# First attention stripes of a four-layer graph stack: the last group's rows, its left and right factors, and the distance behind GpSimd

## The chip, the cores and the metric

The kernel runs on one core of a Trainium2 chip. The metric is the time of one execution on the device in microseconds (us); the median of three runs of the kernel before is 1066.32 us (1062.9 to 1067.3). In this text PE is TensorE (matrix products), DVE is VectorE, ACT is ScalarE, POOL is GpSimd, and SP issues the loads. PSUM is the memory that PE writes its products to, and SBUF is the working memory.

## The reference

A graph of 4096 nodes with 64 features each goes through four layers. The adjacency matrix `adj` (4096 x 4096, zeros and ones) is the same in all of them, and each layer ends in `x = layernorm(x + layer(x))`.

```python
# layer 0: mean over neighbours
h = (adj @ X + X) / clip(sum(adj, 1) + 1, 1)
out = relu(concat([X, h]) @ W + b);  out / max(norm(out), 1e-12)
# layers 1 and 3: hyperbolic attention (curvature c)
left, right = logmap0(x) @ w_att[:D], logmap0(x) @ w_att[D:]
att = sigmoid(left[:, None] + right[None, :] + b_att) * adj
support = einsum('ij,ijd->id', att, logmap(x[:, None], x[None, :]))
proj(expmap(x, support))
# layer 2: a decayed sum over the last neighbours of each row
w = mask * where(pos > 0, 0.5 ** (k - pos), 0);  w @ (x @ weight) + bias
```

In an attention layer every pair of nodes (i receives, j sends) has a weight, which depends on both nodes' rows, and `logmap(x_i, x_j)` is a combination of the two rows whose factors depend on their inner product and norms. So the work by pair is one scalar function of a few inner products, and then a matrix product.

## The kernel before, in words

**Tiles and stripes.** The 4096 nodes form four groups of 1024, taken in the order 3, 2, 1, 0; group 0 is the last. An attention layer has one stripe per group of receiving nodes. A stripe goes through sixteen steps g = 15 to 0, each of two blocks of 128 sending nodes. `load` brings 128 x 2048 values of `adj` for a step (1 MB).

**What a block costs.** For each block, PE fills a PSUM tile z (128 x 1024, two halves of 512, three such tiles in turn) with the sum of three products: the edges (L1143), `hi_lo` of the senders with `lo_hi` of the receivers (L1146), and `src` of the senders with `dst` of the receivers (L1149). ACT makes a sigmoid `sig` (L1161) and a square `sq` of z (L1164). DVE makes the product `t = max(z, 0) * sig` (L1167), and once per step a pass `t = (sq + c) * t` over both blocks, 128 x 2048 (L1170). PE adds t times the rows `xe` to `acc` (L1121), two steps later. `hi_lo` and `src` are called left factors here and `lo_hi` and `dst` right factors: the left ones of a group are used in every stripe, when its nodes send; the right ones only in the group's own stripe. The first stripe (group 3) comes to the senders of group 0 at g = 3, where `need((layer, 0))` asks for them.

**Row work.** Between two layers each group's rows have to be finished and prepared: in layer 0 `end_0` takes the sums by neighbour to rows (matmuls L1510 and L1511, one half of the group at a time or both; L1516 to L1519 finish a half), applies relu (L1523), and normalizes (sums of squares L1525 on POOL and L1527 on DVE, `rsqrt` L775 to L790, scaling and adding L1531 and L1532); `end_2` does the same for layer 2 (L1652 to L1668). Then `norm_rows` applies the layernorm (mean L924 and L925, centring and squares L929 and L930, variance L936 and L938, another `rsqrt`, L944 to L946), and `prepare` makes the factors: b and its reciprocal rb (L958 to L962), the scaled rows y (L967, L968), half-precision copies on ACT (L971 to L973), high and low parts (L975 to L987), `xe` (L994, L997), a third `rsqrt`, and the terms tt and q1 (L1006 to L1008). After that come the four turns, which are transposes on PE (L1023) and a copy on ACT (L1027) each, for hi_lo, lo_hi, src and dst; then two logarithms on ACT (L1031, L1032), the attention matmuls (L1036) and some fifteen small DVE operations, which give `left` and `right` (L1046 to L1073). For group 0 (`pooled` in the code) much of this runs on POOL instead of DVE, so `rsqrt` there is one DVE operation and ten small POOL operations.

**What sets the order.** Row work is written as generators in three queues. `tick` goes through them; it is called after every block and every pass in an attention layer (twice each time in the first stripe of layer 1, four times in that of layer 3), and four times per step in layer 0. A generator that yields n isn't gone on with for n ticks. `soon`, `near`, `after` and `far` give such distances; `far(small, large)` is the distance behind POOL, made from a count of small and of large operations. `need(tag)` ticks until a tag is done. In layers 0 and 2 the order on PE and ACT is that of the program text; in the attention layers the framework's scheduler sets it, and it may move an instruction ahead of the place where the text has it. `take` hands out a PSUM bank for the turns: a second bank (`spare`) is there in layer 0 only, and `spare_ends` closes it before layer 1 begins, when z needs the space. `free` waits until the bank has been given back.

In the kernel before, the last group's `end_0` starts in layer 0, and what is left of it is done under the first stripe of layer 1. The line that decides on one bank or two is

```python
for some in ((0, 1),) if spare else ((0,), (1,)):
```

Of the kernel before, what the change touches and what calls it, by code (L numbers as in the profile page):

```python
# [21 lines left out]
D = 64  # L22
# [39 lines left out]
def gnn_stack_kernel(  # L62
# [509 lines left out]
    def stream(fits):  # L572

        with ExitStack() as st:
# [10 lines left out]
            GROUPS = tuple(reversed(range(NW)))  # L585
# [8 lines left out]
            queues, place, done, held = ([], [], []), [0, 0], set(), []  # L594
# [22 lines left out]
            def tick(n):  # L617
                for _ in range(n):
                    place[1] += 1
                    mark(False)  # L620
                    for queue in queues:
                        while queue and queue[0][1] <= place[1]:
                            wait = next(queue[0][0], None)
                            if wait is None:
                                queue.pop(0)
                                continue
                            queue[0][1] = place[1] + wait
                            if wait:
                                break
                    mark(True)  # L630

            def later(steps, second=False, wait=0):
                queues[int(second)].append([steps, place[1] + wait])
# [10 lines left out]
            def need(tag):  # L644
                while tag not in done:
                    assert any(queues), tag
                    tick(1)
# [12 lines left out]
            def near():  # L660

                return 3 if place[0] == 0 else 1
# [7 lines left out]
            def far(small, large=0):  # L670

                beat = {1: 0.8, 3: 0.4}.get(place[0], 1.6)
                return 1 + int((small * 0.29 + large * 1.04 + 2.3) / beat)

            spare, turn_of = [], [0]

            def take(dtype, *shape):


                held.append(1)  # L680
                turn_of[0] += 1
                if not spare or turn_of[0] % 2:
                    return aux.tile(list(shape), dtype, name="aux")
                return spare[0](dtype, shape)
# [6 lines left out]
            def free():  # L691
                while held:
                    yield 1
# [22 lines left out]
            def grp(name, bufs=None):  # L716
                kw = {"bufs": bufs} if bufs else {}
                return row.tile([P, WB, D], F32, name=name, **kw)

            def nums(name, n=WB):  # L720
                return row.tile([P, n], F32, name=name)
# [81 lines left out]
            src = keep.tile([D + 10, N], F16, name="src")  # L803
# [23 lines left out]
            ys = keep.tile([P, WB, 3 * D + 10], F16, name="ys")  # L827
# [122 lines left out]
            def prepare(layer, s, att, b_att, curve, least, good, small):  # L950
# [5 lines left out]
                pooled = s == GROUPS[-1]  # L956
# [13 lines left out]
                def second():  # L970
# [38 lines left out]
                    by_log = layer == 3 and s != GROUPS[-1]  # L1009
                    if by_log:  # L1010
                        half_log_of_ratio(t, q1)
                    yield far(10, 1) if pooled else 2 * near()
                    for into, rows_of in (
                        (hi_lo, ys[:, :, : 2 * D]),
                        (lo_hi, ys[:, :, D : 3 * D]),
                        (src, ys[:, :, 2 * D :]),
                        (dst, yd),
                    ):
                        n = rows_of.shape[2]
                        yield from free()  # L1020
                        turned = take(F16, P, WW)
                        for k in range(WB):
                            nc.tensor.transpose(  # L1023
                                turned[:n, k * P : (k + 1) * P], rows_of[:, k, :], ident16
                            )
                        yield near()
                        nc.scalar.copy(into[:, cols], turned[:n])  # L1027
                        held.pop()
                        yield 1
                    if not by_log:  # L1030
                        nc.scalar.activation(t, t, AF.Ln, bias=1.0)  # L1031
                        nc.scalar.activation(q1, q1, AF.Ln, bias=1.0, scale=-1.0)  # L1032
# [30 lines left out]
                    if s == GROUPS[0]:  # L1063
                        yield from spread_left(s)
                    done.add((layer, s))

                    V.tensor_mul(own, own, own)
                    V.tensor_mul(g, rbg, rbg)
# [376 lines left out]
            with ExitStack() as lp:  # L1445
# [52 lines left out]
                def end_0(s, tops):  # L1498
                    z = grp("z0")
                    yield from free()  # L1500

                    for some in ((0, 1),) if spare else ((0,), (1,)):
                        ts = []
                        for h in some:
                            top, low = tops[h]
                            t = take(F32, P, SB, P)
                            for k in range(SB):
                                cols = slice(k * P, (k + 1) * P)
                                to = t[:, k, : D + 1]
                                nc.tensor.matmul(to, top[:, cols], sum_w, start=True, stop=False)  # L1510
                                nc.tensor.matmul(to, low[:, cols], count_w, start=False, stop=True)  # L1511
                            ts.append((h, t))
                        for h, t in ts:
                            at = slice(s * WB + h * SB, s * WB + (h + 1) * SB)
                            d = nums("deg", SB)
                            V.reciprocal(d, t[:, :, D])  # L1516
                            zz = z[:, h * SB : (h + 1) * SB, :]
                            V.tensor_mul(zz, t[:, :, :D], over(d))
                            V.tensor_add(zz, zz, xw[:, at, :])  # L1519
                        if some == (0,):  # L1520
                            yield near()
                    held.clear()
                    V.tensor_scalar(z, z, 0.0, None, ALU.max)  # L1523
                    sq, n2 = grp("sq"), nums("n2")
                    nc.gpsimd.tensor_mul(sq, z, z)  # L1525
                    yield 1
                    V.tensor_reduce(n2, sq, AX.X, ALU.add)  # L1527
                    V.tensor_scalar(n2, n2, 1e-24, None, ALU.max)
                    if s == GROUPS[-1]:
                        n = yield from Small(True, "").rsqrt(n2, "n", 0)  # L1530
                        nc.gpsimd.tensor_mul(z, z, over(n))  # L1531
                        nc.gpsimd.tensor_add(z, z, x0[:, blocks(s), :])  # L1532
                        yield far(10, 2)
                    else:
                        n = rsqrt(n2, "n")
                        yield 1
                        V.tensor_mul(z, z, over(n))
                        V.tensor_add(z, z, x0[:, blocks(s), :])
                        yield 1
                    yield from norm_rows(1, s, z, x2[:, blocks(s)])  # L1540
                    yield from prepare(
                        1, s, att1, batt1_sb, curve1, 1e-15, good[:, 0], 70
                    )

                with tc.manual_schedule(engines=FIXED):
                    for s in GROUPS:
                        sums = [ps.tile([P, W], F32, name="acc") for _ in range(2)]
                        counts = [ps.tile([P, W], F32, name="acc") for _ in range(2)]
                        parts = ((first, sums, P), (third, counts, D + 1))
# [34 lines left out]
                        for h in range(2):  # L1584
# [9 lines left out]
                            nc.scalar.copy(low, counts[h][: D + 1])  # L1594
                            tops.append((top, low))
                        later(end_0(s, tops))
                        if s > 0:
                            own_of = linear(0, s - 1, w0_sb[:D, :], own_part)
                            later(in_turn((0, s - 1), own_of))
# [11 lines left out]
            def attention(layer, curve, rates, behind):  # L1611

                need((layer, GROUPS[0]))
                for n, s in enumerate(GROUPS):
                    if n:
                        need((layer, s, "left"))
                    anchored[0] = n > 0
                    then = GROUPS[n + 1] if n + 1 < NW else None
                    sums = attend(layer, s, rates[n], then)
                    move_s = in_turn((layer, s, "moved"), move(layer, s, sums, curve))  # L1620
                    if n:
                        later(
                            in_turn((layer + 1, s + 1), there((layer, s + 1, "moved")), behind(s + 1)),
                            True, 9,
                        )
                    apart = 2 if n + 1 == NW and layer == 1 else 0
                    later(move_s, apart)
                    if n + 1 == NW:
                        later(in_turn((layer + 1, s), behind(s)), apart)
                anchored[0] = False  # L1630
# [188 lines left out]
            into = aux.tile([D, 1], F32, name="aux")  # L1819
# [22 lines left out]
    with tc.If(fit < P):  # L1842
        with ExitStack() as st:
# [6 lines left out]
            for t, w_att in ((att1_sb, w_att1), (att3_sb, w_att3)):  # L1850
                src = w_att.rearrange("a o -> o a")
# [38 lines left out]
```

## Time and profile before

| | us |
|---|---|
| median of three runs | 1066.32 |
| profiled execution, its own time | 1064.98 |
| its span in the profile | 1063.3 |
| stretch of layer 1's first stripe, from 186.30 | to 270.40 |
| group 0's row work on DVE in layer 3, from 718.48 | to 761.25 |
| one step of a later stripe, two products and a pass on DVE | 2 x 1.22 + 2.31 |

The busiest engine over the whole span is PE (93%), then DVE (85%), ACT (71%) and POOL (32%). Of the 40 slices of the span, each 26.6 us long, PE is below nine tenths in the first, the fourth, the seventh to the ninth (159.5 to 239.2 us), the twenty-eighth (717.7 to 744.3 us) and the last. A share of the span is a mean over four layers with different limits, so the question here is what the engines do in two places: from 186 us, where layer 1 begins, and from 715 us, where layer 3 does. In the views below, one line of the timeline is: start, duration, engine, line of the code, operation, result and operands with their shapes, how many of them, and in brackets the idle time before it and who ended that. A line of the waits is: what waited, for what, total, times, longest.

### The profile page before, as it was taken

Reading aid. Unit: us, or ns where it says so; the run is one execution under the profiler, and the core shown is the slowest. Engines: PE = TensorE matmul, PEld = TensorE weight load, DVE = VectorE, ACT = ScalarE, POOL = GpSimd, SP = SyncE. Lnnn points to the kernel's source line nnn. Section 1 sums busy time; section 2 is a strip of 40 time slices with the busy share of each in tenths; the row PEclk is TensorE's granted clock in tenths of the full one; section 3 lists DMA queues with packets and bytes.
Section 4 is the critical chain, followed back from the end, with each engine's and each line's share of the span. In section 5 each row is a group of like instructions: output and inputs, shape, how many; then the busy total and the mean of one; then the engine's idle time right before and its main releaser. Section 6 shows DMA issues by size and latency. Waiting matters only on the chain.

```text
span 1063.3 us, 13594 instructions
## 1 busy us (share of the span) xinstructions
PE 985.4 (93%) x4845; PEld 400.7 (38%) x4845; DVE 901.2 (85%) x1383; ACT 753.4 (71%) x876; POOL 339.1 (32%) x695
## 2 busy tenths in 40 slices
PE   4998998879999999999999999997999999999991
PEld 2454554323333333333333344442333333333330
DVE  6677878779999999999485579857899999999996
ACT  0013122859989888888677688896998888888970
POOL 0011222470064464455200020105401562573670
PEclk8999999989999999999999999998999999999996
DMA  8999999836665656566599999994465766665600
GB/s 338 369 420 367 389 390 387 336 107 222 216 220 198 238 204 232 198 224 219 218 331 341 372 357 314 322 328 179 163 240 194 245 226 209 237 218 198 228 3 22
DMA packets 38580, 271.62 MB, mean 255 GB/s; under 512 B 4710, under 2 KB 4710, under 8 KB 5734
## 3 DMA queue, kind: packets, MB, share of 16 engines
q1 hardware_dynamic: 37728, 270.03, 69.7%
q8 instruction: 40, 0.66, 0.2%
q10 hardware_dynamic: 774, 0.63, 0.2%
q14 instruction: 38, 0.31, 0.1%
HBM read 269.58 MB, written 1.05 MB: 255 GB/s over the span
## 4 chain that ended last, share of the span: by engine, by line
PE 66%; DVE 18%; POOL 5%; DMA 4%; ACT 4%; issue 2%; ACTq 0%; SPq 0%; POOLq 0%; DVEq 0%
PE acc L1121 18%; PE z L1743 11%; PE z L1143 8%; PE z L1149 8%; PE z L1146 7%; DVE t L1170 5%; DVE t L1167 5%; PE acc L1561 4%; DMA edges<-in_adj_dram 3%; PE z L1755 3%; DVE junk L871 2%; PE z L1709 2%; ACT sq L1750 1%; ACT sq L1164 1%; POOL sq L1525 1%
## 5 line engine op out<-in xcount | busy, mean ns | idle before, releaser
L1167 DVE SCALAR_TENSOR_TENSOR t<-z,sig 128x1024 f32<-128x1024 f32 x256 | 309.1, 1218 | 22.4 <-ACT sq L1164 19.8
L1164 ACT ACTIVATE sq<-z 128x1024 f32<-128x1024 f32 x256 | 255.4, 1022 | 62.1 <-PE z L1149 31.7
L1170 DVE SCALAR_TENSOR_TENSOR t<-sq,t 128x2048 f32<-128x2048 f32 x127 | 293.4, 2311 | 0.3
L1161 ACT ACTIVATE sig<-left_b,right 128x1024 f32<-128x1024 f32 x256 | 287.3, 1150 | 6.5 <-DVE t L1167 6.0
L1121 PE MATMUL acc<-t,xe 128*64 128x512 f32 x1024 | 261.5, 616 | 13.4 <-DVE t L1170 13.4
L1143 PE MATMUL z<-edges,two_i 128*128 128x512 bf16 x512 | 200.3, 391 | 6.2 <-DVE t L1167 6.2
L1149 PE MATMUL z<-dst,src 74*128 74x512 f16 x512 | 194.8, 380 | 0.0
L1146 PE MATMUL z<-lo_hi,hi_lo 128*128 128x512 f16 x512 | 193.7, 378 | 0.0
L1750 ACT ACTIVATE sq<-z 128x512 bf16<-128x512 f32 (+1 forms) x192 | 137.9, 741 | 39.5 <-PE z L1743 38.8
L1121 PEld LDWEIGHTS acc<-t,xe 128*64 128x64 f32 x1024 | 64.9, 138 | 144.4 <-issue 110.0
L871 DVE SCALAR_TENSOR_TENSOR t<-edges 128x2048 bf16<-128x2048 f32 x32 | 74.4, 2335 | 28.7 <-DMA edges<-in_adj_dram 28.6
L1561 PE MATMUL acc<-edges,first 128*128 128x512 bf16 x256 | 81.1, 398 | 18.1 <-DMA edges<-in_adj_dram 17.9
L1143 PEld LDWEIGHTS <-two_i 128*128 128x128 bf16 x512 | 50.3, 98 | 118.7 <-issue 73.1
L1743 PE MATMUL z<-edges,pass_by 128*128 128x512 bf16 x248 | 86.4, 388 | 6.3 <-ACT sq L1750 5.8
L1743 PE MATMUL z<-edges,enter 128*128 128x512 bf16 x256 | 88.2, 387 | 0.0
L871 DVE SCALAR_TENSOR_TENSOR junk<-edges 128x2048 bf16<-128x2048 f32 x32 | 73.1, 2284 | 14.9 <-DMA edges<-in_adj_dram 14.9
L1561 PE MATMUL acc<-edges,third 128*65 128x512 bf16 x256 | 80.5, 396 | 0.0
L1149 PEld LDWEIGHTS <-src 74*128 74x128 f16 x512 | 49.1, 96 | 73.5 <-issue 11.9
L1146 PEld LDWEIGHTS <-hi_lo 128*128 128x128 f16 x512 | 50.2, 98 | 63.7 <-issue 18.3
L1270 POOL TENSOR_TENSOR w_att<-x,u 128x512 f32<-128x512 f32 x6 | 18.2, 3028 | 169.9 <-ACT u L1264 169.9
L1709 PE MATMUL z<-sq,halves 128*128 128x512 bf16 x128 | 48.1, 377 | 0.6 <-ACT sq L1750 0.6
L1525 POOL TENSOR_TENSOR sq<-z 128x512 f32<-128x512 f32 x4 | 10.1, 2526 | 117.2 <-DVE z L1523 97.4
(466 smaller groups left out, 996.5 us busy)
## 6 DMA issues: line engine op xcount, KB each, us to landing
edges<-in_adj_dram SPq DMA_DIRECT2D x256, 1024.0 KB, 4.9
x<-in_x_dram SPq DMA_DIRECT2D x4, 256.0 KB
out_dram<-x ACTq DMA_DIRECT2D x2, 256.0 KB
out_dram<-x SPq DMA_DIRECT2D x2, 256.0 KB
w_sb<-in_L_gnn_W_dram ACTq DMA_DIRECT2D x1, 32.0 KB, 4.9
w_twice<-in_L_gnn_weight_dram ACTq DMA_DIRECT2D x2, 16.0 KB, 8.7
given<-in_L_gnn_b_dram ACTq DMA_DIRECT2D x1, 0.2 KB
given<-in_L_gnn_bias_dram ACTq DMA_DIRECT2D x1, 0.2 KB
```

The lines of the kernel that those rows point to most:

```text
L871: V.scalar_tensor_tensor(junk, a, 0.0, a, ALU.not_equal, ALU.not_equal, accum_out=odd[:, n : n + 1])
L1121: it = nc.tensor.matmul(acc[h * D : (h + 1) * D, :], xe[:, j, :], t[:, k, h * W : (h + 1) * W], start=j == BLOCKS[0], stop=j == BLOCKS[-1],)
L1143: nc.tensor.matmul(half, two_i, edge[:, at : at + W], start=True, stop=False)
L1146: nc.tensor.matmul(half, hi_lo[:, of], lo_hi[:, to], start=False, stop=False)
L1149: last = nc.tensor.matmul(half, src[:, of], dst[:, to], start=False, stop=True)
L1161: nc.scalar.activation(sig, left_b, AF.Sigmoid, bias=right[:, j : j + 1])
L1164: nc.scalar.activation(sq[:, k], zp, AF.Square, bias=ROOT + OFF, scale=-1.0 / UNIT)
L1167: V.scalar_tensor_tensor(ts[k][:, k], zp, 0.0, sig, ALU.max, ALU.mult)
L1170: V.scalar_tensor_tensor(t, sq, HIGH**2, t, ALU.add, ALU.mult)
L1561: nc.tensor.matmul(accs[h][:m], lhs[:, j, :], edge[:, at : at + W], start=j == BLOCKS[0], stop=j == BLOCKS[-1],)
L1743: nc.tensor.matmul(z[:, h : h + W], lhs, rhs[:, h : h + W], start=j == BLOCKS[0], stop=True, skip_group_check=True,)
L1750: weighed[0] = nc.scalar.activation(w, z[:, :n], AF.Exp, bias=-(OFF_EDGE + CUT) * LN2, scale=-LN2)
```

## The change

- The last group's `end_0` in layer 0 is now driven until both halves of its rows are out of PSUM (a new tag, `(0, s, "rows")`, and a `need` for it) while both banks are still there.
- The order of the four turns becomes hi_lo, src, lo_hi, dst, for all groups. For group 0 only the left factors, hi_lo and src, are turned at that place. Its logarithms, attention matmuls and terms follow, then the tag that the first stripe asks for; the right factors lo_hi and dst are turned behind it. A new tag, "turned", is asked for ahead of every stripe but the first.
- The distance `far` grows: its constant goes from 2.3 to 3.9 us, which is one tick more in layers 0 and 2, two in layer 1 and four in layer 3. Ahead of the turns its arguments go from 10 small and 1 large operations to 14 and 2.

```diff
@@ -670,7 +670,7 @@
             def far(small, large=0):
 
                 beat = {1: 0.8, 3: 0.4}.get(place[0], 1.6)
-                return 1 + int((small * 0.29 + large * 1.04 + 2.3) / beat)
+                return 1 + int((small * 0.29 + large * 1.04 + 3.9) / beat)
 
             spare, turn_of = [], [0]
 
@@ -1009,13 +1009,15 @@
                     by_log = layer == 3 and s != GROUPS[-1]
                     if by_log:
                         half_log_of_ratio(t, q1)
-                    yield far(10, 1) if pooled else 2 * near()
-                    for into, rows_of in (
+                    yield far(14, 2) if pooled else 2 * near()
+                    turns = [
                         (hi_lo, ys[:, :, : 2 * D]),
+                        (src, ys[:, :, 2 * D :]),
                         (lo_hi, ys[:, :, D : 3 * D]),
-                        (src, ys[:, :, 2 * D :]),
                         (dst, yd),
-                    ):
+                    ]
+
+                    def turn(into, rows_of):
                         n = rows_of.shape[2]
                         yield from free()
                         turned = take(F16, P, WW)
@@ -1027,6 +1029,9 @@
                         nc.scalar.copy(into[:, cols], turned[:n])
                         held.pop()
                         yield 1
+
+                    for parts in turns[:2] if pooled else turns:
+                        yield from turn(*parts)
                     if not by_log:
                         nc.scalar.activation(t, t, AF.Ln, bias=1.0)
                         nc.scalar.activation(q1, q1, AF.Ln, bias=1.0, scale=-1.0)
@@ -1063,6 +1068,10 @@
                     if s == GROUPS[0]:
                         yield from spread_left(s)
                     done.add((layer, s))
+                    if pooled:
+                        for parts in turns[2:]:
+                            yield from turn(*parts)
+                    done.add((layer, s, "turned"))
 
                     V.tensor_mul(own, own, own)
                     V.tensor_mul(g, rbg, rbg)
@@ -1520,6 +1529,7 @@
                         if some == (0,):
                             yield near()
                     held.clear()
+                    done.add((0, s, "rows"))
                     V.tensor_scalar(z, z, 0.0, None, ALU.max)
                     sq, n2 = grp("sq"), nums("n2")
                     nc.gpsimd.tensor_mul(sq, z, z)
@@ -1594,6 +1604,8 @@
                             nc.scalar.copy(low, counts[h][: D + 1])
                             tops.append((top, low))
                         later(end_0(s, tops))
+                        if s == GROUPS[-1]:
+                            need((0, s, "rows"))
                         if s > 0:
                             own_of = linear(0, s - 1, w0_sb[:D, :], own_part)
                             later(in_turn((0, s - 1), own_of))
@@ -1613,6 +1625,7 @@
                 need((layer, GROUPS[0]))
                 for n, s in enumerate(GROUPS):
                     if n:
+                        need((layer, s, "turned"))
                         need((layer, s, "left"))
                     anchored[0] = n > 0
                     then = GROUPS[n + 1] if n + 1 < NW else None
```

## The prediction

> **What bounds the kernel now.** I read the page's head, then the busy times of four stretches, then the waits and the timeline of the two that are not full. The head says that TensorE is the bound over the whole:
>
> ```profile
> span 1063.3 us, 13594 instructions
> PE 985.4 (93%) x4845; PEld 400.7 (38%) x4845; DVE 901.2 (85%) x1383; ACT 753.4 (71%) x876; POOL 339.1 (32%) x695
> ```
>
> The edits act where the two attention layers begin. Busy times by stretch (first stripe of layer 1, a later stretch of it, then the same for layer 3):
>
> ```profile
> core 0: us, PE busy (x) PEld busy (x) DVE busy (x) ACT busy (x) POOL busy (x), PEclk, DMA share, GB/s
> 186.30:270.40 84.10, 73.15 (x361) 28.98 (x362) 68.71 (x90) 69.32 (x74) 32.01 (x56) 0.96 0.59 213
> 270.40:347.00 76.60, 76.60 (x336) 27.15 (x335) 74.47 (x55) 67.91 (x73) 31.12 (x79) 1.00 0.63 218
> 720.00:790.00 70.00, 61.37 (x284) 22.48 (x283) 60.93 (x73) 58.77 (x64) 24.57 (x43) 0.95 0.55 193
> 790.00:870.00 80.00, 80.00 (x351) 28.14 (x349) 78.03 (x58) 71.16 (x75) 29.45 (x78) 1.00 0.61 211
> ```
>
> Later stretches have no PE idle at clock 1.00. The first stripes have 10.95 us (84.10 - 73.15) and 8.63 us, at 0.96 and 0.95: about 19.6 us is all that this change can address, plus the slow clock. PE there waits for DVE's products, and DVE for GpSimd. DVE's waits in 181 to 290 us (total, times, longest):
>
> ```profile
> DVE t L1167 <- ACT sq L1164: 6.8, 6, 4.0
> DVE rb L962 <- POOL b L959: 2.2, 1, 2.2
> DVE n_m L924 <- POOL z L1532: 2.1, 1, 2.1
> DVE n_v L936 <- POOL sq L930: 0.9, 1, 0.9
> ```
>
> The timeline, layer 1 and then layer 3, shows the chain behind them:
>
> ```profile
> 199.54 2.28 POOL L787 TENSOR_TENSOR rs_t<-n 128x8 f32<-128x8 f32 x1
> ...
> 230.44 1.03 PE L1023 MATMUL aux<-ident,ys 128*128 128x128 f16 x8 [4.14 <-POOL ys L987]
> 231.40 3.68 PE L1121 MATMUL acc<-t,xe 128*64 128x512 f32 x8
> ...
> 238.17 1.22 DVE L1167 SCALAR_TENSOR_TENSOR t<-z,sig 128x1024 f32<-128x1024 f32 x1 [4.02 <-ACT sq L1164]
> ...
> 737.57 0.20 DVE L962 RECIPROCAL rb<-b 128x8 f32<-128x8 f32 x1 [3.70 <-POOL b L959]
> ...
> 739.98 1.97 PE L1121 MATMUL acc<-t,xe 128*64 128x512 f32 x4 [3.82 <-DVE t L1170]
> ...
> 757.45 0.17 DVE L1054 SCALAR_TENSOR_TENSOR f<-q,tt 128x8 f32<-128x8 f32 x1 [1.30 <-ACT q L1032]
> ```
>
> PE's 4.14 us wait for ys becomes, a few instructions later, DVE's 4.02. GpSimd's small operation took 2.28 us instead of 0.20 because it lay under a DVE pass (L1170 at 199.48, also 2.28). Read off the timeline after product 0 (products are numbered from 0 in issue order), DVE idles 0.36 + 2.14 + 0.93 + 2.23 + 4.02 + 1.19 + 0.26 + 0.30 + 0.72 = 12.15 us in layer 1, and 1.22 + 3.70 + 0.40 + 1.30 + 0.74 + 0.99 = 8.35 us in layer 3. PE has no gap after 255.57 and 766.24.
>
> **What the Trainium skill says.** "SBUF — State Buffer", "SBUF: two separate sides": DVE and GpSimd share a port pair under a lock held for a whole instruction, so a DVE operation with two SBUF inputs shuts GpSimd out. The trace agrees (2.28 for 0.20). "TensorE: Matmul & The Clock Gate", "What's actually happening": the clock halves after some 3.4 us of idleness. Agrees: after 4.14 us idle the accumulation (L1121) takes 3.68 us for a usual 1.94, the next z block 1.23 for 0.66, 2.3 us more; after 3.82 us in layer 3 the same. "ScalarE: Activation LUTs", "What ACT_TABLE_LOAD costs": about 1.28 us for a load; the trace has 1.28 ahead of L1031. "PSUM — Partial Sum Buffer", "PSUM bank collisions raise a hardware error": engines on one bank are put in order. Agrees: sq ran 191.34 to 192.37, its product began at 192.40.
>
> **The change part by part.** What follows rests on the order in which each engine of the changed program issues its instructions, with the durations of the trace before. The counts are the same; nothing is removed but waits, and no DMA moves.
>
> Costing nothing: hi_lo, src before lo_hi, dst in layers 0 and 2 (the same 8 transposes and one 1.0 us copy each, under a PE that is full; exposed they would be equal too); the wait for "turned" of later groups (group 0's is turned by the tenth of a stripe's 16 steps, three stripes early); one tick more in layer 0.
>
> Layer 1, against before:
> 1. *Both halves from two banks.* The second half's matmuls (L1510/1511) now precede the first z block; they wait for ACT's last src copy (185.4). z starts at about 188.2 instead of 186.44, product 0 at 191.25 instead of 190.49: +0.76. Row operations that lay after product 0 (relu 0.34, n 0.60 net of overlap) leave, but some 0.2 returns as a longer sq wait: -0.75.
> 2. *L924 right behind product 0* (before: after product 4). GpSimd's ten rsqrt operations and two wide ones now have one product and no other cover; I get their end at 196.6, so the wait grows from 2.14 to 4.2: +2.06. PE idles about 4.5 us here, and its clock drops, but DVE is ahead with nothing yet owed.
> 3. *L936 after product 4*: its 0.93 goes. L962 keeps its two products and two passes of cover: 2.2, no change.
> 4. *Distance and order at the transposes.* ys's low part (L987) stands 3.6 us earlier on GpSimd, hi_lo's transposes (8, L1023) later: PE's 4.14 becomes 1.9, and the 4.02 of DVE goes: -4.02.
> 5. *Terms ahead of right factors.* Ln (L1031) now comes before the sq of product 16, and needs GpSimd's last small operation (L1007), which by the walk just misses a gap and lies under a pass: ACT stops, sq is behind it, DVE idles: +1.9. Product 17's 1.19 stays. The three small ones (1.28) become 0.35: -0.93.
>
> Sum: 0.76 - 0.75 + 2.06 - 0.93 - 4.02 + 1.9 - 0.93 = -1.9. The miss in step 5 is by 0.2 to 0.3 us, less than the walk's error; without it the 1.9 is gone and half of the 1.19: -4.4. I take the middle, -3.1.
>
> Layer 3: L936's 1.22 goes (product 3 is ahead of it); L962 has two products and a pass more of other work on DVE, 3.70 becomes 1.7: -2.0; 0.40 goes. Ln stands before the sq of product 14 and its input ends at about 758.85 while the table is loaded by 755.2: DVE waits 3.0 in place of 1.30: +1.7. The attention matmuls (L1036) need the one row bank that src's copy (763.45) still holds; z blocks are queued behind them on PE, which idles about 4.8; of this DVE sees 1.6 where it waited 0.74 + 0.99: -0.1. PE's slow clock then costs 2.3, of which I let 1.5 reach the end. Sum -1.2 - 2.0 - 0.4 + 1.7 - 0.1 + 1.5 = -0.5. Bounds: -5.0 without the Ln wait and the slow clock, +1.5 if the L962 wait stays. Group 0's left factors are needed at product 24; all this is done some four products earlier, so nothing is late next.
>
> Together -3.6: the profiled execution (1064.98, span 1063.3) would take 1061.4; it stood 1.3 below the median of the runs, so the median goes from 1066.32 to 1062.7. A measurement of this kernel can tell about 0.5% from no change: 1061.0 and 1071.7 are the marks.
>
> **Rivals.** *A, the chain slips between the passes.* No Ln wait in either layer: -4.4 - 5.0 = -9.4, 1056.9. For it: passes are only 2.28 of each 4.62 us step, and the early L987; against: eleven small operations in a row, each of which can meet a pass. *B, the slower side: GpSimd's lock, moved onto ACT.* Each further small operation under a pass costs 2.28 - 0.20 = 2.1, and where Ln waits, every later sq is behind it, with nothing in between. From the two sums (-2.4), one more collision is about even with before, and four more, two in each layer, pass the mark: +6.0, 1072.3. For it: the Ln waits are new, and L924 lost its cover. Against: collisions also go away with the order. *C, waits only change their names:* the row chain on GpSimd is as long as before, and where product 24 isn't waiting for it, distance without a shorter chain gives back later what it saves (4.02 saved, 2.06 + 1.9 paid): 1066. Against it: PE loses its slow stretch in layer 1's transposes.
>
> **How the numbers follow.** Forecast 0.34, A 0.30, C 0.16, B 0.20. Faster than 1061.0: nearly all of A (0.28) and the low edge of the forecast (0.08), 0.36. Slower: B, 0.19. The rest, 0.45. The range, 1055 to 1072, leaves out A's lowest tenth or two and half of B; the forecast's own is 1060 to 1065.5.
>
> **What would show it.** Right: the L924 wait near 4 us, no L936 wait, PE at L1023 (hi_lo, layer 1) below 2.5 us and L1121 behind it at 1.94, no 4 us wait of L1167; in layer 3 L962 near 1.7; new waits of ACT for L1007. Wrong towards A: no ACT waits for L1007, a first stripe of layer 3 with PE idle under 5 us. Wrong towards B: several GpSimd operations of 128x8 at about 2.3 us ahead of Ln, PE idle above 11 us in a first stripe. A change outside 181 to 256 and 718 to 778 us would overturn the whole.

## The result, and the profile after

| | before | after |
|---|---|---|
| median of 21 runs, us | 1066.99 (1062.9 to 1072.2) | 1062.45 (1059.0 to 1067.5) |
| profiled execution: own time, span, us | 1064.98, 1063.3 | 1063.81, 1062.1 |

The ratio of after to before is 0.9957, 95% interval 0.9942 to 0.9971: the change makes the kernel faster by 4.5 us, with 3.6 forecast. The two profiled executions stand only 1.2 us apart, and that difference has to be understood before anything is read from it. First the head of the page of after:

```profile
span 1062.1 us, 13509 instructions
PE 981.6 (92%) x4760; PEld 401.9 (38%) x4845; DVE 900.2 (85%) x1383; ACT 753.1 (71%) x876; POOL 339.0 (32%) x695
```

The counts of DVE, ACT and POOL are those of before. (PE has 85 records fewer, but as many weight loads: matmul records that are missing from the trace.) Then the busy times of the two first stripes, in the stretches that were shown of before:

```profile
core 0: us, PE busy (x) PEld busy (x) DVE busy (x) ACT busy (x) POOL busy (x), PEclk, DMA share, GB/s
186.30:270.40 84.10, 75.47 (x357) 29.24 (x364) 70.86 (x91) 71.59 (x77) 34.04 (x56) 0.94 0.61 221
720.00:790.00 70.00, 62.62 (x283) 23.32 (x287) 61.86 (x74) 59.64 (x64) 24.60 (x43) 0.95 0.53 185
```

PE's idle time went from 10.95 to 8.63 us and from 8.63 to 7.38 us, but its clock in layer 1 from 0.96 to 0.94: some idleness has become slow running. DVE's waits in 181 to 290 us, after:

```profile
DVE t L1176 <- ACT sq L1173: 5.2, 7, 1.6
DVE n_m L924 <- POOL z L1542: 3.8, 1, 3.8
DVE rb L962 <- POOL b L959: 2.2, 1, 2.2
```

The wait of L936 is gone, and the longest wait for a square fell from 4.0 to 1.6 us; L924's has grown from 2.1 to 3.8. (Behind the edit at L1009 the line numbers are up to 13 higher than before: the product L1167 is L1176 here, the pass L1170 is L1179, the turns L1023 are L1025, the logarithm L1031 is L1036.) The timeline of after, first layer 1 on PE, ACT and POOL, then layer 3:

```profile
198.67 0.61 PE L1152 MATMUL z<-edges,two_i 128*128 128x512 bf16 x1 [3.56 <-DVE t L1176]
...
201.35 3.05 PE L1130 MATMUL acc<-t,xe 128*64 128x512 f32 x8
...
225.59 0.40 PE L1025 MATMUL aux<-ident,ys 128*128 128x128 f16 x4 [1.51 <-POOL ys L987]
225.91 1.94 PE L1130 MATMUL acc<-t,xe 128*64 128x512 f32 x8
...
236.20 2.33 POOL L1006 TENSOR_TENSOR tt<-q,rt 128x8 f32<-128x8 f32 x1
...
238.89 0.21 ACT L1036 ACTIVATE tt<-tt 128x8 f32<-128x8 f32 x1 [2.24 <-POOL tt L1007]
...
739.16 0.20 DVE L962 RECIPROCAL rb<-b 128x8 f32<-128x8 f32 x1 [1.37 <-POOL b L959]
...
757.91 0.21 ACT L1036 ACTIVATE tt<-tt 128x8 f32<-128x8 f32 x1 [3.02 <-POOL tt L1007]
...
762.53 0.34 PE L1041 MATMUL aux<-att,hi_lo 128*128 128x7 bf16 x8 [2.90 <-ACT src L1029]
```

PE's wait for ys at the turns went from 4.14 to 1.51 us, and the accumulation behind it from 3.68 to 1.94. The slow stretch has moved to 198 us, behind L924, where PE idles 3.56 us and the accumulation takes 3.05. On ACT the logarithm now waits for GpSimd, 2.24 and 3.02 us, behind a small operation (L1006) that lay under a pass; in layer 3 the attention matmuls wait 2.90 us for the row bank.

To see where the two executions part, I compare the start of corresponding DVE passes and ACT squares. Against before, the end of layer 0 (first copy of the last group's sums, 182.48 before) is 0.41 us earlier, the table load just ahead of the first square of layer 2 (512.13) 2.87 us earlier, the last square of layer 2 (713.91) 0.59 us later, and the 101st pass (909.62, layer 3, past its first stripe) 0.32 us earlier; the rest of the 1.2 us lies behind that. So layer 1 gained 2.5 us, layer 3 0.9, and layer 2, where the change moves two turns at most, lost 3.5. All of that loss falls at 540 us. GpSimd and DVE in layer 2, after and then before:

```profile
540.42 3.28 POOL L1404 TENSOR_TENSOR x_hl<-x,x_hl 128x512 f16<-128x512 f32 x1 [30.22 <-ACT x_hl L1403]
540.40 2.29 DVE L871 SCALAR_TENSOR_TENSOR t<-edges 128x2048 bf16<-128x2048 f32 x1 [0.76 <-DMA edges<-in_adj_dram]
543.76 0.62 PE L1409 MATMUL aux<-ident,x_hl 128*128 128x128 f16 x8 [2.14 <-DVE un L756]
```

```profile
543.30 1.16 POOL L1395 TENSOR_TENSOR x_hl<-x,x_hl 128x512 f16<-128x512 f32 x1 [30.22 <-ACT x_hl L1394]
543.35 3.26 DVE L871 SCALAR_TENSOR_TENSOR t<-edges 128x2048 bf16<-128x2048 f32 x1 [0.84 <-DMA edges<-in_adj_dram]
```

Before, GpSimd's subtraction started 0.05 us ahead of a DVE pass over edges that had just landed; it took 1.16 us, and the pass was stretched to 3.26. After, the pass was 0.02 us ahead, GpSimd took 3.28 us, and PE, whose order in layer 2 is fixed, stood before the transposes. The view names DVE L756 as the one that ended PE's wait; but the matmul starts at 543.76, right after GpSimd's end (540.42 + 3.28 = 543.70). Behind the wait PE ran slowly for some microseconds (a group of eight products L1768 took 1.92 us where the others take 1.05).

### The profile page after: what moved, and what is told of

Same layout as the page of the kernel before. It is cut to its first block, busy times and chain, and to the rows that moved or that the text cites. A ratio compares the mean times of both kernels' runs of the same rounds, so it can differ in the third digit from the quotient of the medians.

```text
span 1062.1 us, 13509 instructions
## 1 busy us (share of the span) xinstructions
PE 981.6 (92%) x4760; PEld 401.9 (38%) x4845; DVE 900.2 (85%) x1383; ACT 753.1 (71%) x876; POOL 339.0 (32%) x695
## 3 DMA queue, kind: packets, MB, share of 16 engines
HBM read 269.58 MB, written 1.05 MB: 255 GB/s over the span
## 4 chain that ended last, share of the span: by engine, by line
PE 62%; DVE 21%; ACT 6%; POOL 6%; issue 2%; DMA 2%; ACTq 0%; SPq 0%; POOLq 0%; DVEq 0%
PE acc L1130 16%; PE z L1756 11%; PE z L1155 7%; PE z L1158 7%; PE z L1152 7%; DVE t L1179 6%; DVE t L1176 6%; PE acc L1571 5%; PE z L1768 3%; DVE junk L871 2%; PE z L1722 2%; DMA edges<-in_adj_dram 2%; ACT sq L1173 2%; ACT sq L1763 1%; POOL sq L1535 1%
## 5 line engine op out<-in xcount | busy, mean ns | idle before, releaser
L1176 DVE SCALAR_TENSOR_TENSOR t<-z,sig 128x1024 f32<-128x1024 f32 x256 | 309.1, 1219 | 22.4 <-ACT sq L1173 20.1
L1179 DVE SCALAR_TENSOR_TENSOR t<-sq,t 128x2048 f32<-128x2048 f32 x127 | 293.3, 2309 | 0.3
L1170 ACT ACTIVATE sig<-left_b,right 128x1024 f32<-128x1024 f32 x256 | 286.6, 1149 | 3.6 <-DVE t L1176 3.2
L1152 PE MATMUL z<-edges,two_i 128*128 128x512 bf16 x463 | 181.8, 393 | 5.8 <-DVE t L1176 5.8
L1571 PE MATMUL acc<-edges,first 128*128 128x512 bf16 x241 | 77.9, 400 | 16.8 <-DMA edges<-in_adj_dram 16.3
L1722 PE MATMUL z<-sq,halves 128*128 128x512 bf16 x122 | 45.9, 377 | 0.8 <-ACT sq L1763 0.6
```

The costliest lines, as they stand in the source:

```text
L1152: nc.tensor.matmul(half, two_i, edge[:, at : at + W], start=True, stop=False)
L1170: nc.scalar.activation(sig, left_b, AF.Sigmoid, bias=right[:, j : j + 1])
L1176: V.scalar_tensor_tensor(ts[k][:, k], zp, 0.0, sig, ALU.max, ALU.mult)
L1179: V.scalar_tensor_tensor(t, sq, HIGH**2, t, ALU.add, ALU.mult)
L1571: nc.tensor.matmul(accs[h][:m], lhs[:, j, :], edge[:, at : at + W], start=j == BLOCKS[0], stop=j == BLOCKS[-1],)
```

## The experiments

Three questions are asked: which of the three parts makes the gain, what the other two cost, and what happened in layer 2. Each profile gives the same three sums against before: layer 1 from the end of layer 0 to the table load ahead of the first square of layer 2, layer 2 from there to its last square, layer 3 from there to the 101st pass. All kernels compute the whole function. (The expectations name -2.3, -4.2 and -7.6 for layer 1 where the table has -2.5, -4.1 and -7.7; such tenths aren't read.) The end of layer 0 alone, which waits for edges, lay between 1.6 us earlier and 3.5 us later.

A star in the table below marks a sum with a slow clock that cost time: behind one wait TensorE ran slowly, and behind the same wait in another kernel of the table it did not. In layer 1, the last kernel and the one three lines above it have the same order, and both wait 1.98 us ahead of the same accumulation. It takes 1.94 us in the upper one (first line) and 3.16 in the last (second line):

```profile
230.40 1.94 PE L1123 MATMUL acc<-t,xe 128*64 128x512 f32 x8 [1.98 <-DVE t L1172]
...
230.70 3.16 PE L1123 MATMUL acc<-t,xe 128*64 128x512 f32 x8 [1.98 <-DVE t L1172]
```

In layer 3, the changed kernel and the two that only move subtractions do the same up to the wait of 2.90 us at the attention matmuls (762.53 above). In the stretch that begins with these matmuls the clock (third figure from the end) was 0.87 in the changed kernel, shown first, and 1.00 in the one with the last group's subtraction on DVE:

```profile
762.00:775.00 13.00, 11.58 (x61) 5.12 (x61) 9.19 (x16) 10.88 (x12) 0.00 (x0) 0.87 0.40 127
```

```profile
760.54 0.34 PE L1041 MATMUL aux<-att,hi_lo 128*128 128x7 bf16 x8 [2.90 <-ACT src L1029]
...
760.00:773.00 13.00, 11.59 (x69) 4.97 (x69) 10.65 (x17) 12.31 (x14) 0.00 (x0) 1.00 0.45 163
```

A star is worth 1.7 us in layer 1 (-7.5 and -5.8), about 1.4 in layer 2 and 1.6 in layer 3 (-2.5 and -0.9). Where order and star are the same, the sums repeat to 0.4 us. A difference under 1.7 us is read only where the clock behind the waits has been compared. What lets the clock fall in one execution and not in another, the runs don't show. A kernel's median is over many executions, so it needn't agree with the sums of its one profile.

| kernel | ratio to before (95%) | layer 1 | layer 2 | layer 3 |
|---|---|---|---|---|
| the changed kernel | 0.9957 (0.9942 to 0.9971) | -2.5 | +3.5* | -0.9* |
| early rows only | 0.9984 (0.9966 to 1.0001) | -1.6 | +3.4* | +0.1 |
| order only | 1.0003 (0.9984 to 1.0023) | -0.6 | +3.5* | -0.6 |
| distance only | 0.9888 (0.9860 to 0.9916) | -7.7 | +0.3 | -4.5 |
| changed, without early rows | 0.9933 (0.9913 to 0.9953) | -6.1* | +2.3 | -0.8* |
| changed, without the order | 0.9913 (0.9886 to 0.9941) | -4.1 | +2.1 | -4.5 |
| changed, logarithms later | 0.9898 (0.9867 to 0.9929) | -4.4 | +2.0 | -5.1 |
| changed, mean held back | 0.9987 (0.9961 to 1.0012) | +0.1 | 0.0 | -0.9* |
| changed, last group's subtraction on DVE | 0.9947 (0.9928 to 0.9967) | -2.8 | -0.3 | -2.5 |
| early rows, distance, mean and reciprocal held back | 0.9897 (0.9862 to 0.9932) | -7.5 | 0.0 | -4.6 |
| distance only, last group's subtraction on DVE | 0.9912 (0.9889 to 0.9936) | -7.8 | +3.5* | -4.5 |
| changed, two subtractions on DVE | 0.9921 (0.9898 to 0.9944) | -2.8 | -0.4 | -1.0* |
| early rows, distance, held back as above, two subtractions on DVE | 0.9847 (0.9800 to 0.9893) | -5.8* | -0.4 | -4.5 |

**One part alone.** A theory, D, and two rivals to it, R and O, stand in the first expectations. The three parts of the change, each put into the kernel before. The first:

```diff
                     held.clear()
+                    done.add((0, s, "rows"))
...
                         later(end_0(s, tops))
+                        if s == GROUPS[-1]:
+                            need((0, s, "rows"))
```

> The kernel before with only the first part: both halves of the last group's rows out of PSUM while both banks are there. Milestone: start of the eleventh pass (L1170) of layer 1 against the kernel before, corrected by the end of layer 0; and the same at the eleventh pass of layer 3 against the start of layer 3. Theory D (the distance makes the gain, the early rows cost): L924 waits near 4 us behind product 0 instead of 2.1, so layer 1 is 1 to 3 us slower; layer 3 0. Rival R (the early rows make the gain, since the row chain starts earlier): layer 1 is 2 us faster or more, layer 3 0.

The second: `turns`, `turn`, the terms ahead of the right factors and "turned", as in the change.

> Only the second part: left factors first, logarithms and terms ahead of the right factors. Theory D: the wait for ys ahead of hi_lo's turn stays near 4 us, the logarithm waits for GpSimd on ACT in addition, layer 1 between 0 and +2 us, layer 3 between 0 and +2. Rival O (the order makes the gain, since terms no longer wait behind four turns): both layers 1 us faster or more.

The third:

```diff
-                return 1 + int((small * 0.29 + large * 1.04 + 2.3) / beat)
+                return 1 + int((small * 0.29 + large * 1.04 + 3.9) / beat)
...
-                    yield far(10, 1) if pooled else 2 * near()
+                    yield far(14, 2) if pooled else 2 * near()
```

> Only the third part: the longer distance. Theory D: L924 and L936 find GpSimd done or nearly (2.1 and 0.9 us go), the wait for ys halves and the 4.0 us wait of L1167 goes; layer 1 -4 to -6 us, layer 3 -2 to -3.5 us. Rivals R and O: within 1 us of before in layer 1; without the earlier start the longer distance would push group 0's terms against product 24.

And the change without its first part:

> The changed kernel without its first part (order and distance only). Theory D: layer 1 -3 to -5 us against before, better than the changed kernel's -2.3; layer 3 as the changed kernel, about -0.9. Rival R: layer 1 worse than the changed kernel, by 1 us or more.

The distance alone gives more than the whole change: -7.7 and -4.5 us, more than any theory had for either layer, and a median of 1054.84. (Which of its waits, all lengthened at once, brings how much isn't separated.) Its waits of PE in 183 to 290 us, and its first stripe:

```profile
PE acc L1121 <- DVE t L1170: 5.4, 6, 2.0
PE aux L1023 <- POOL ys L987: 1.5, 1, 1.5
```

```profile
189.30:265.70 76.40, 68.84 (x349) 27.60 (x353) 67.56 (x88) 67.31 (x71) 29.79 (x56) 1.00 0.64 231
```

PE still idles 7.56 us, but never over 2.0 us at once, and its clock stays at 1.00. L924 stands one product later and waits 1.0 us, L962 waits 0.8, and L936 doesn't wait.

The early rows alone were a miss for theory D: -1.6 us where +1 to +3 were expected, and a ratio whose interval just reaches 1. L924 does wait as theory D says, but the wait for ys, which was put down to the distance, went as well; DVE's and PE's waits of that kernel:

```profile
DVE n_m L924 <- POOL z L1533: 4.3, 1, 4.3
...
PE aux L1023 <- POOL ys L987: 0.2, 1, 0.2
```

The order alone, with -0.6 in both layers and a ratio of 1.0003, is between theory D (0 to +2) and rival O (-1 or more), nearer to no effect than to either; it removes none of the waits (ys 4.1, L924 2.1, L936 0.9), and the logarithm's wait for GpSimd that theory D expected isn't there. The gains of the parts, -1.6, -0.6 and -7.7 in layer 1, don't add up to the -2.5 of the whole: without the early rows the change gains 6.1 there, more than theory D's 3 to 5, and by the size of a star it would be some 7.8 at full clock, as with the distance alone: in layer 1 the order costs nothing that can be read there. The early rows, alone a small gain at most, cost 3.6 us or more in layer 1 beside the longer distance (-6.1 and -2.5; the ratios, 0.9933 and 0.9957, agree in sign, but their intervals overlap): both remove the wait for ys, and the early rows bring a longer one at L924. The same 3.6 us stand between the distance alone (-7.7) and the next kernel (-4.1), both without the order. Rivals R and O fall.

**What the order and the early rows cost.**

> The changed kernel with the turns and terms in their old order (early rows and distance only). If the new order is what costs in layer 3, its gain there is that of the distance alone, -4.6 us, instead of -0.9; in layer 1 the early rows remain, so -3 to -5 us, against -2.3 for the changed kernel and -7.6 for the distance alone. If the order is innocent: -0.9 and -2.3.

Layer 3 is back at -4.5 us: beside the longer distance the order costs 3.6 us there, about 2 of them at full clock (-2.5 with the last group's subtraction on DVE) and the rest the slow clock behind its wait of 2.90 us. In layer 1 -4.1 stands within the expected range, with a wait of 3.9 us at L924 and 3.6 us on PE. The next kernel keeps the order and only lets the logarithms wait:

```diff
+                    if pooled:
+                        yield {1: 4, 3: 8}[layer]
                     if not by_log:
                         nc.scalar.activation(t, t, AF.Ln, bias=1.0)
```

> The changed kernel with its new order, but the two logarithms and what follows held back by two products (4 ticks in layer 1, 8 in layer 3) for the last group. If the logarithm's wait for GpSimd on ACT and the attention matmuls' wait for the row bank are what the order costs: those waits (2.2 and 3.0 us on ACT, 2.9 us on PE) fall below 0.5, layer 1 goes from -2.3 to about -4, layer 3 from -0.9 to between -3 and -4.6. If it is the order of the turns itself: both stay within 0.7 us.

Layer 3 went to -5.1 and layer 1 to -4.4. In layer 3 of the changed kernel, PE's and ACT's waits were

```profile
PE aux L1041 <- ACT src L1029: 2.9, 1, 2.9
...
ACT tt L1036 <- POOL tt L1007: 3.0, 1, 3.0
```

and with the logarithms later

```profile
PE aux L1043 <- ACT src L1029: 0.3, 1, 0.3
...
ACT tt L1038 <- POOL tt L1007: 1.0, 1, 1.0
```

(1.0 and not below 0.5 as expected.) The slow clock at this place is gone as well. So it isn't the order of the turns that costs, but that logarithms and attention matmuls follow the left factors with no distance of their own. Which of the two waits costs more in layer 3 is open: the edit moves both.

For the early rows:

```diff
-                V.tensor_reduce(m, v, AX.X, ALU.add)
+                mean = V.tensor_reduce(m, v, AX.X, ALU.add)
+                if s == GROUPS[-1] and layer == 1:
+                    in_order(mean.ins, pairs_last[mybir.EngineType.DVE])
...
-                        yield far(10, 2)
+                        yield far(10, 2) + 4
```

> The changed kernel, with the mean of the last group's rows in layer 1 (L924) held behind the products already issued, and 4 ticks more ahead of it: it then stands behind product 2 and the first pass instead of product 0. If its 3.8 us wait and the slow clock behind it are what the early rows cost: the wait falls below 0.7, the clock stays at 1.00, layer 1 goes from -2.3 to between -4 and -6 us; layer 3 as the changed kernel. If the early rows cost elsewhere (the later start of layer 1), or the pass takes the port from GpSimd and gives it back: layer 1 within 1 us of -2.3.

This failed on both theories: L924's wait left the list, the reciprocal's fell to 1.4, and layer 1 got worse, +0.1. What is late next is the end of the row chain: on ACT the logarithm now stood right behind hi_lo's copy, ahead of src's. Waits of PE and ACT in that kernel's layer 1:

```profile
PE aux L1043 <- ACT src L1031: 3.1, 1, 3.1
...
ACT tt L1038 <- POOL tt L1009: 3.8, 1, 3.8
```

DVE's waits for squares rose to 11.0 us (5.2 in the changed kernel). A test of the early rows has to be made without the new order, and it moves the reciprocal too (the mean is held as above):

```diff
-                        yield far(10, 2)
+                        yield far(10, 2) + 2
...
-                    yield far(14, 1)
+                    yield far(14, 1) + (3 if layer == 1 else 0)
```

> Early rows and distance with the old order of turns, as in the run without the new order (layer 1 -4.2 us), and for the last group in layer 1: the mean (L924) held behind the products already issued with 2 ticks more ahead of it, and 3 ticks more ahead of the reciprocal (L962 there). They then stand behind the first pass and behind pass 4. If the 3.9 us wait of the mean and the 2.2 us wait of the reciprocal are what the early rows cost, both fall below 1 us, the clock stays at 1.00, and layer 1 is between -6.5 and -9 us, layer 3 -4.5. If the early rows cost by the later start of layer 1 or a longer chain, layer 1 stays within 1 us of -4.2.

Layer 1 went from -4.1 to -7.5 us; the mean waits 1.2 us, a little over the expectation, the reciprocal not at all, and the clock in 183 to 261 us is 1.00. A later kernel with the same order in layer 1 had -5.8, and the difference is the star described above. So these two waits are where the early rows cost, by the sums of layer 1; which of the two, the edit can't tell, and the ratios of the kernels with and without them (0.9897 and 0.9913) are too close to add anything. Over the distance alone, whose layer 1 is -7.7, nothing is gained: without those waits the early rows make no difference that can be read.

**The race in layer 2.** In the profiles with GpSimd doing this subtraction, it took 1.15 or 1.16 us in five (layer 2: -0.3 to +0.3 us) and 3.12 to 3.28 us in seven (+2.0 to +3.5). In all twelve the one that started first kept its own length: the pass in the seven, ahead by 0.02 to 0.19 us, and GpSimd in the five, ahead by 0.02 to 1.60 (at 1.60 the two no longer overlap). In the seven PE waited 1.99 to 2.14 us. Behind that wait its clock over 12 us was 0.86 in four (+3.4 to +3.5, the stars) and 1.00 in three (+2.0 to +2.3). The length of the wait doesn't separate them: 2.05 us is among the four, 2.06 among the three. Two kernels were meant to take it off GpSimd:

```diff
-                nc.gpsimd.tensor_sub(hl[:, :, D:], xg, hl[:, :, :D])
+                (V if s == GROUPS[-1] else nc.gpsimd).tensor_sub(
+                    hl[:, :, D:], xg, hl[:, :, :D]
+                )
```

> The changed kernel with one operation of layer 2 moved: the last group's subtraction for its halves (L1404) on DVE instead of GpSimd. In the profile it took 3.28 us in the changed kernel, having started 0.02 us after a DVE pass over edges, and 1.16 us in the kernel before, 0.05 us ahead of one; layer 2 was 3.5 us longer in the changed kernel. If a race between the two by some hundredths of a microsecond decides over these 3.5 us in each execution: layer 2 as short as in the kernel before, the slower half of the executions goes, the median is 1.5 to 3.5 us below the changed kernel's 1062.5 and the spread of the executions is smaller. If that was one execution's chance: the same median.

> The distance alone, with the last group's subtraction in layer 2 on DVE. Layer 1 -7.6 and layer 3 -4.5 us as with the distance alone, layer 2 within 0.5 us of the kernel before's in every execution; median near 1054, about 1 us below the distance alone.

They say nothing on the race, because the edit took the wrong group's: the subtraction at 540 us is that of the group before the last. It stayed on GpSimd, with 1.15 us in the first kernel and 3.21 in the second, and layer 2 came out at -0.3 and at +3.5. With `s in GROUPS[-2:]`:

> The changed kernel with the subtraction for the halves on DVE for the last two groups in layer 2. The two earlier runs of this kind had moved only the last group's (at 568 us); the one that races with a DVE pass (at 540 us) is that of the group before it. If the race decides over the length of layer 2: no wait of PE for the halves at about 540 us, layer 2 within 0.5 us of the kernel before's, median 1 to 3 us below the changed kernel's 1062.5. If it is not the race: layer 2 again up to 3.5 us longer, the same median.

> The run with early rows, distance, the old order and the held mean, with the two subtractions on DVE in addition. Layer 1 -7.5 and layer 3 -4.5 us as there, layer 2 within 0.5 us of the kernel before's; median about 1053.5, 9 us below the changed kernel and 13 below the kernel before.

Layer 2 was at -0.4 in both, and PE's wait at 540 us is gone. The ratio of the changed kernel went from 0.9957 to 0.9921, but the two intervals just touch. How often the race goes which way in the kernel before can't be told from its one profile. The last kernel has the lowest median: 1052.68 us, 1.5% below the kernel before. Its interval overlaps that of the distance alone, so that it is faster than that isn't shown.

## Why the prediction was right, and where not

The ways in which the change gains and costs are those that were forecast, most of them to a few tenths. That the median fits to 0.3 us (1062.7 forecast, 1062.45 measured) is in part luck. The forecast had nothing for the race in layer 2, which moves a single execution by 2 to 3.5 us, and over 21 runs the median before is 1066.99 and not 1066.32, so that the change is 4.5 us where 3.6 were forecast. The sums of the two stages, -3.1 and -0.5, came out as -2.5 and -0.9 in the one profile; -3.1 was the middle of two cases, and the one that came had been put at -1.9. By its steps:

- *Step 1, both halves early.* z starts at 188.14 as said (188.2), product 0 at 191.64 instead of 191.25. Since layer 0 ended 0.41 us earlier, the delay is 1.56 us and not 0.76. Product 0 was released by its square, and that stood behind a first z block that took 2.36 us where before it took 1.48: PE ran slowly there. In four other kernels with the early rows (early rows only, logarithms later, and the two that only move subtractions) that block is at full clock, and the delay is 0.81 or 0.82. The term was right; the slow block came on top.
- *Step 2, L924 behind product 0.* 3.82 us measured, 4.2 forecast; PE's idle time 3.56 for 4.5, with the slow clock. In the four kernels just named the two are 4.24 to 4.26 and 4.42 to 4.45. The slow clock there costs next to nothing, as the prediction had it: the accumulation behind it took 3.05, 3.68 and 2.44 us in the changed kernel and the two that only move subtractions, and layer 1 is -2.5, -2.8 and -2.8.
- *Step 3.* L936's wait is gone; L962's is 2.22 (2.2 forecast).
- *Step 4, the transposes.* 1.51 us for 1.9; the 4.02 us wait is gone, and the accumulation takes 1.94.
- *Step 5, the logarithm.* Of the two cases the one with the wait came: ACT waits 2.24 us, DVE 1.57 (1.9 forecast) and 1.35 at the next product (1.19).
- *Layer 3.* L936's wait gone; L962 1.37 (1.7); ACT's wait for GpSimd 3.02, of which DVE saw 1.85 and not 3.0. PE idled 2.9 us at the attention matmuls, not 4.8, and DVE 1.72 (1.6). The 1.5 us for a slow clock came: at full clock DVE's later wait of 1.27 us for a square isn't there, and layer 3 is 1.6 us shorter. Not forecast was one more wait for a square, of 1.56 us (1.36 at full clock), which took up what the smaller wait at the logarithm left.

One statement did not hold: that a change outside the two stages would overturn the whole. Layer 2 did change, by 3.5 us, from a race that the order of the instructions doesn't show, and a slow clock behind it; it hid most of the gain in the profiled pair, and says nothing against the steps. Of the rivals, A's time (1056.9) was reached, but by the kernel with the logarithms later (1055.7) and not by this change, which has the logarithm's wait in both layers. B's mechanism is there at the size that the sum had given it: in layer 1 two small operations of the last chain ahead of the logarithm lie under a pass (L786 2.35 us and L1006 2.33), where before one did (L779 2.25). C was right on two of the three parts, whose waits only move.

What the prediction missed is how the parts stand to each other. It entered +2.06 in step 2 and +1.9 in step 5 as the price of the whole; the runs show them to be the price of two parts, which bring nothing readable that the third doesn't bring alone.

## What to carry to other kernels

When several edits remove the same wait, cost each of them alone before the sum: here one part alone was worth 12 us, and with the other two beside it 4.5 were left. Operations that follow on a moved step need a distance of their own; moved ahead, they carried the wait for GpSimd onto ACT, where every square stands behind it. Before two profiles are compared by their spans, compare them by layers: a difference in a layer that the edit hardly touches is a matter of its own. And before a difference of one or two microseconds between single profiles is given to an edit, compare the clock behind each wait: here it alone made 1.4 to 1.7 us.

## What the runs showed of the hardware

- Of a DVE pass and a wide GpSimd operation, the one that starts first keeps its own length and the other is stretched, and a lead of 0.02 us is enough: with the pass ahead, GpSimd took 3.28 us instead of 1.16; with GpSimd ahead, the pass took 3.28 instead of 2.29 (early rows, distance, mean and reciprocal held back). That the first one keeps the port for its whole length is what the Trainium skill states ("SBUF — State Buffer", "SBUF: two separate sides"); the twelve profiles agree. That so small a lead decides over 2 us of a 1063 us kernel, and over 3.5 with the slow clock behind it, was the surprise. DVE had slack at this place, and PE had none.
- Behind the same wait TensorE ran at full speed in one kernel and slowly in another: 1.98 us in layer 1 (accumulation 1.94 and 3.16), 2.06 and 2.05 us in layer 2 (clock 1.00 and 0.86), 2.90 us in layer 3 (1.00 and 0.87). So the length of a wait doesn't decide alone. Nor does a slow clock always cost: behind 1.31 us at the start of layer 3, the accumulation took 3.47 us with the distance alone and 1.94 with the mean and reciprocal held back, and layer 3 is -4.5 and -4.6. The Trainium skill ("TensorE: Matmul & The Clock Gate", "What's actually happening") has a window that runs free of the kernel, which fits that, but asks for a whole idle window of about 3.4 us, and these waits were shorter.
